# Attention with a mixture of experts: tokens of twelve batches loaded a second time in squares and turned by VectorE, with the norm moved into weights and copies

## The chip, the cores and the metric

One core of one Trainium2 chip. The metric is the device time of one execution in microseconds. The engines named below are TensorE (PE; its weight loads are PEld), VectorE (DVE), ScalarE (ACT), GpSimd (POOL) and SyncE (SP), which here only issues transfers.

## What is computed

Tokens x (16 batches of 512 tokens, 128 channels, fp32) are normalised over the channels. The result goes both through causal attention with 16 heads of 8 channels, whose queries and keys are scaled to length one, and through 8 experts of which each token uses the best two. Both are added to x.

```python
xn = (x - mean(x)) / sqrt(var(x) + 1e-5)
# attention
q, k, v = heads(xn @ Wq), heads(xn @ Wk), heads(xn @ Wv)
sim = (l2norm(q) @ l2norm(k).T) * 8.0            # causal
attn = (softmax(sim) @ v) @ Wo
# experts
probs = softmax(xn @ Wr.T); top_v, top_i = top_k(probs, 2)
w_e = where(top_i == e, top_v / sum(top_v), 0)
ffn = sum_e(w_e * (gelu(xn @ W1[e].T + b1[e]) @ W2[e].T + b2[e]))
out = x + attn + ffn
```

## The kernel before

**Order.** From line 1027 on, the instructions of PE, DVE, ACT and SP run in the order in which the program writes them (`manual_schedule`); `on_pool` (line 562) does the same for POOL. What is written before that line (loads of x and of weights, constants) is placed by the scheduler. An engine that waits holds up all that is written behind it on that engine.

**Stages.** The attention of a batch is ten stages (`PER`), 160 in all. `stage` (line 1175) writes for each: the scores of this stage (`scores`, line 725: PE matmuls `sim`, ScalarE exponentials `ex`), one step of the list `side` (line 1141), the causal masks due, the products with v of an earlier stage (`weigh`, line 772, into the PSUM tile `av`), and the steps that `at_stage` has booked for stage t. Preparing a batch (`prep`, line 622) is booked into the stages before it: four projections (`proj`, line 628), squares and their sums, the length (`root`), the scaling, the turns of q and k (`turn_q`, `turn_k`) and the four masked copies of k (`alone`).

**Tokens.** `load_x` (line 100) brings a batch as [128 tokens, 4, 128 channels]; SP issues all sixteen first. `stats` (line 225) takes mean and variance of each token on VectorE, `scales` (line 252) makes `rstd` and `shift`, and `normalise` (line 289) writes `rows`, the normalised tokens, on ScalarE or GpSimd. Matmuls need them with channels on the partitions: `turn_x` (line 302) turns four 128x128 blocks on PE into a PSUM bank, and a copy brings the bank to `xnT[b]`. Batches 0 to 2 are turned ahead of stage 0; `turn(3)` to `turn(15)` are steps of `side` in stages 0 to 18, with VectorE as the copier. `proj` multiplies a block of `xnT[b]` with `wall` (Wq, Wk and Wv side by side) and lets ScalarE copy the result to `qkv`. `logits` (line 311) multiplies `xnT` of four batches with `wr_sb`, and VectorE copies the result to `ltT`; `turn_logits` turns it back and writes `lg`. `logits(0)` is the sixth step of `side`, `logits(4)` the eighth. `rows` is also what GpSimd later scatters into `slots`, the expert's input, from stage 40 on.

**Buffers.** `misc` (line 191) is one PSUM bank shared by turns, projections, logits and others. `SIM` uses one of three double banks. `scratch` (line 220) hands out two SBUF buffers in turn; its users are, in the order of writing, `count_up` (line 1044), `fill` (line 1071), then `ltT` of `logits(0)`, `ltT` of `logits(4)`, and so on.

**SP's queue.** After the sixteen loads of x, SP issues 45 stores of the tile `fill` to `slots` in HBM (line 1075), 24 copies that pack the experts' weights (line 1084), the store and load of the counts (line 424), and from line 865 on, for each block of the experts, four loads `z<-slots` and one `w<-packed`. `z` is loaded in squares: tokens 32 at a time on 32 partitions, pieces of 32 channels, 128 bytes each, so that VectorE's transpose of 32x32 squares turns it (`turn_rows`, line 882).

**Idle work.** `keep_busy` (line 1058) lets PE do matmuls on a tile of zeros.

```python
    def scratch(name, n):

        return rs.tile([P, NB * E], F32, tag="scratch", name=name, bufs=2)[:, :n]
```

Of the kernel before, what the change touches and what calls it, by code (L numbers as in the profile page):

```python
# [10 lines left out]
F32 = mybir.dt.float32  # L11
I32 = mybir.dt.int32
AF = mybir.ActivationFunctionType
ALU = mybir.AluOpType
# [10 lines left out]
def attention_moe_kernel(  # L25
# [19 lines left out]
    nc = tc.nc  # L45
    B, S, D = x.shape
    E = wrT.shape[1]
    M = w1T.shape[2]
    P = 128
    NC = S // P  # L50
# [3 lines left out]
    TB = 32  # L54
    NQKV = 3 * D
    NG = 4
    GB = 4
# [4 lines left out]
    NT = B * NC  # L62
# [15 lines left out]
    for k in range(E - 1):  # L78
# [9 lines left out]
    keep = ctx.enter_context(tc.tile_pool(name="keep", bufs=1))  # L88

    xnT2 = [  # L90
        keep.tile([P, 2, S], F32, tag=f"xnT{b}", name=f"xnT{b}") for b in range(0, B, 2)
    ]
# [7 lines left out]
    def load_x(b):  # L100
        t = keep.tile([P, NC, D], F32, tag=f"x{b}", name=f"x{b}")
        nc.sync.dma_start(t, x[b].rearrange("(c p) d -> p c d", p=P))
        x_sb.append(t)

    wall = const.tile([P, NQKV], F32, name="wall")
    wr_sb = const.tile([P, 32], F32, name="wr_sb")
# [5 lines left out]
        nc.scalar.dma_start(wall[:, n * D : (n + 1) * D], w)  # L112
    nc.scalar.dma_start(wo_sb, wo)
    nc.scalar.dma_start(b1_sb, b1T)
    for b in range(B):
        load_x(b)

# [45 lines left out]
        channel_multiplier=0,  # L165
    )

    xnT = [xnT2[b // 2][:, b % 2] for b in range(B)]

    pos = keep.tile([P, 2, NT], I32, name="pos")  # L170

# [19 lines left out]
    def misc(name):  # L191
        return ps_m.tile([P, 512], F32, tag="misc", name=name)

    def SIM(name):
        return ps_sim.tile([P, 2, S], F32, tag="sim", name=name)[:, 0]
# [4 lines left out]
    ]  # L200


    rctx = ExitStack()
    rs = rctx.enter_context(tc.tile_pool(name="rs", bufs=1))
    rows_all = rs.tile([P, NT, ROW], F32, name="rows")
    rows = [rows_all[:, b * NC : (b + 1) * NC] for b in range(B)]
    lg = rs.tile([P, NT, E], F32, name="lg")
    wsel = rs.tile([P, 2, NT], F32, name="wsel")
    sels = [rs.tile([P, NT, E], F32, tag=f"sel{k}", name=f"sel{k}") for k in range(2)]
    st = rs.tile([P, NT, 6], F32, name="st")  # L210
    rstd = rs.tile([P, NT], F32, name="rstd")
    shift = rs.tile([P, NT], F32, name="shift")
    ones = rs.tile([P, P], F32, name="ones")
    upper = rs.tile([P, P], F32, name="upper")
# [74 lines left out]
    def normalise(b, engines):  # L289

        for c, engine in enumerate(engines):
            i = b * NC + c
            to, what = rows[b][:, c, :D], x_sb[b][:, c]
            by, less = rstd[:, i : i + 1], shift[:, i : i + 1]
            if engine is nc.scalar:
                nc.scalar.activation(to, what, AF.Identity, bias=less, scale=by)
            elif engine is nc.vector:
                nc.vector.tensor_scalar(to, what, by, less, ALU.mult, ALU.add)
            else:
                on_pool(nc.gpsimd.tensor_scalar, to, what, by, less, ALU.mult, ALU.add)  # L300

    def turn_x(b, bank, copy):

        for c in range(NC):
            nc.tensor.transpose(bank[:, ts(c, P)], rows[b][:, c, :D], ident)
        copy(xnT[b], bank)  # L306


    turned = {}

# [10 lines left out]
    def turn_logits(b0):  # L321
        ltT = turned.pop(b0)
        pt = misc(f"lg{b0}")
        for c in range(NC):
            nc.tensor.transpose(pt[:, ts(c, P)], ltT[:, ts(c, P)], ident)
        nc.vector.tensor_copy(
            lg[:, b0 * NC : (b0 + GB) * NC].rearrange("p (g c) e -> p c g e", g=GB),
            pt.rearrange("p (c g w) -> p c g w", g=GB, w=32)[:, :, :, :E],
        )

    def route():

# [289 lines left out]
    def prep(b):  # L622

        t0 = PER * b
        s = live[b] = {}
        s["vaug"] = vaugs[b % 2]

        def proj(c, bank=misc):
            if not c:
                s["qkv"] = p2.tile([P, NC, NQKV], F32, tag="qkv", name=f"qkv{b}")  # L630
            pp = bank(f"proj{b}_{c}")
            nc.tensor.matmul(  # L632
                pp[:, :NQKV], xnT[b][:, ts(c, P)], wall, start=True, stop=True
            )
            nc.scalar.copy(s["qkv"][:, c], pp[:, :NQKV])  # L635

        heads = lambda t: t.rearrange("p c (h d) -> p c h d", d=DH)

        def squares(c):
            if not c:  # L640
                s["qkn"] = p1.tile([P, NC, 2 * D], F32, tag="qkn", name=f"qkn{b}")
            qk = s["qkv"][:, c, : 2 * D]
            on_pool(nc.gpsimd.tensor_mul, s["qkn"][:, c], qk, qk)

        def values(c):
            on_pool(
                nc.gpsimd.tensor_copy,
                s["vaug"][:, c : c + 2, :, 0:DH],
                heads(s["qkv"][:, c : c + 2, 2 * D : 3 * D]),
            )  # L650

        n = NC * 2 * HEADS

        def sums():
            s["ss"] = sm.tile([P, n], F32, tag="ss", name=f"ss{b}", bufs=1)
            nc.vector.tensor_reduce(
                s["ss"].rearrange("p (c h) -> p c h", c=NC), heads(s["qkn"]), AX.X, ALU.add
            )
            nc.vector.tensor_scalar_max(s["ss"], s["ss"], L2_EPS * L2_EPS)

        def root_now(meanwhile):

            s["rn"] = sm.tile([P, n], F32, tag="rn", name=f"rn{b}", bufs=1)
            nc.scalar.activation(s["ss"], s["ss"], AF.Sqrt)
            meanwhile()
            nc.vector.reciprocal(s["rn"], s["ss"])

        def root():

            s["rn"] = sm.tile([P, n], F32, tag="rn", name=f"rn{b}", bufs=1)  # L670
            (by_log if b < B - 1 else guess)(s["rn"], s["ss"])

        def root_step():
            t = sm.tile([P, n], F32, tag="t", name=f"t{b}")
            refine(s["rn"], s["ss"], t, 1 if b < B - 1 else 3)

        def scale():
            nc.vector.tensor_mul(
                heads(s["qkn"]),
                heads(s["qkv"][:, :, : 2 * D]),  # L680
                s["rn"].rearrange("p (c h) -> p c h", c=NC).unsqueeze(3).to_broadcast(
                    [P, NC, 2 * HEADS, DH]
                ),
            )

        def turn_q():
            pt = misc(f"qt{b}")
            for c in range(NC):
                nc.tensor.transpose(pt[:, ts(c, P)], s["qkn"][:, c, :D], ident)  # L689
            s["qT"] = p2.tile([P, S], F32, tag="qT", name=f"qT{b}")  # L690
            nc.vector.tensor_copy(s["qT"], pt)

        def turn_k(bank=misc):
            pt = bank(f"kt{b}")
            for c in range(NC):
                nc.tensor.transpose(pt[:, ts(c, P)], s["qkn"][:, c, D:], ident)  # L696
            s["kr"] = p1.tile([P, S], F32, tag="turned", name=f"kr{b}")
            nc.vector.tensor_copy(s["kr"], pt)

        def alone(r):  # L700

            if not r:
                s["kT"] = p2.tile([P, NG, S], F32, tag="kT", name=f"kT{b}")
            nc.vector.tensor_scalar_mul(s["kT"][:, r], s["kr"], hmask[:, r : r + 1])  # L704

        if not b:
            return SimpleNamespace(
                proj=proj, squares=squares, values=values, sums=sums, root_now=root_now,
                scale=scale, turn_q=turn_q, turn_k=turn_k, alone=alone,
            )  # L710
        times = (-18, -17, -14, -11) if b > 1 else (-11, -11, -10, -9)
        for c, t in enumerate(times):
            at_stage(t0 + t, lambda c=c: proj(c, SIM if t0 + t < 0 and c else misc))
        for t, step in (
            (-11, lambda: squares(0)), (-11, lambda: squares(1)),
            (-10 + (b == 1), lambda: squares(2)), (-9 + (b == 1), lambda: squares(3)),
            (-8, lambda: values(0)),
            (-7, lambda: values(2)), (-7, sums), (-6, root),
            (-5, root_step), (-4, scale), (-3, turn_q), (-2, turn_k),
            (-2, lambda: alone(0)), (-1, lambda: alone(1)), (0, lambda: alone(2)),  # L720
            (b != B - 1, lambda: alone(3)),
        ):
            at_stage(t0 + t, step)
# [321 lines left out]
    first = 0  # L1045
# [12 lines left out]
    def keep_busy(n, what=spare):  # L1058

        for _ in range(n):  # L1060
            nc.tensor.matmul(
                misc("idle")[:, : what.shape[1]], what[:, :P], what, start=True, stop=True
            )

    keep_busy(4)
    stats(0)
    for step in scales(0, 1, True):
        step()
# [3 lines left out]
    nc.gpsimd.memset(fill, 0.0)  # L1072
    nc.gpsimd.memset(fill[:, :, D : D + 1], float(2 * T))
    for k in range(NFILL):
        nc.sync.dma_start(
            slots[k * P * NR : (k + 1) * P * NR].rearrange("(p r) w -> p r w", r=NR),
            fill,
        )
# [11 lines left out]
    ACT, POOL, DVE = nc.scalar, nc.gpsimd, nc.vector  # L1090
    zero = prep(0)
    normalise(0, (ACT, ACT, DVE, DVE))
    turn_x(0, SIM("xnt0"), nc.scalar.copy)
    for b in range(1, 4):
        stats(b)
# [40 lines left out]


    def turn(b):
        turn_x(b, misc(f"xnt{b}"), nc.vector.tensor_copy)

    side = [
        lambda step=step, b=b: step(b)
# [88 lines left out]
    t = PER * B  # L1231
# [48 lines left out]
```

## Time and profile before

| | us |
|---|---|
| median of 3 runs | 757.83 |
| lowest, highest | 748.12, 759.42 |
| the profiled execution | 759.72 |
| its span in the trace | 757.9 |

| engine, in the whole span | busy us | instructions |
|---|---|---|
| TensorE | 718.6 | 6270 |
| VectorE | 478.1 | 1066 |
| ScalarE | 468.1 | 732 |
| GpSimd | 458.3 | 545 |

The chain of waits is read from its last instruction back: at each step to what released it, so its lines are where the time of the whole went. A line of a timeline or of the chain begins with the start and the length in microseconds. In a table by windows each line has the stretch, its length, the busy time of PE, PEld, DVE, ACT and POOL with the number of instructions, the granted PE clock, the mean busy share of the 16 DMA engines and the rate in GB/s; the share can pass 1 when packets of one engine overlap. `SPq` or `DVEq` is the sequencer of an engine, which also shows semaphore waits. The stages of attention run from about 24 us to 440 us and again from about 690 us; between lie the blocks of the experts.

### The profile page before, as it was taken

How to read it: one execution, taken by the hardware profiler on the slowest of the kernel's cores; microseconds unless marked ns; L12 is line 12 of the kernel's file. 1: busy time of each engine (PE TensorE's matmuls, PEld its weight loads, DVE VectorE, ACT ScalarE, POOL GpSimd, SP SyncE). 2: the span in 40 equal slices, each digit the busy share in tenths (PEclk: the TensorE clock that was granted, in tenths of full speed). 3: DMA queues.
4: the chain of work that ended last, by engine and by line, in shares of the span. 5: the costliest groups of instructions: out<-in, count | busy, mean ns of one | idle time of the engine just before them, and what ended most of it. 6: DMA issues, size and time to landing. Idle time of an engine off the chain costs nothing.

```text
span 757.9 us, 16860 instructions
## 1 busy us (share of the span) xinstructions
PE 718.6 (95%) x6270; PEld 431.9 (57%) x6270; DVE 478.1 (63%) x1066; ACT 468.1 (62%) x732; POOL 458.3 (60%) x545
## 2 busy tenths in 40 slices
PE   8899999999999899998999997999989999999996
PEld 3344444343444344443443476898989999989442
DVE  8855679888777577564675753545455444544487
ACT  4777687777778477776786752444434444344873
POOL 5667455489888587785778423555545555546453
PEclk9999999999999899998999998999999999999999
DMA  9993000010110011110101398999988999893793
GB/s 263 336 266 107 1 2 1 3 37 31 37 37 29 30 34 33 34 37 23 37 30 34 68 160 196 250 252 253 244 215 227 236 244 239 236 238 105 230 339 108
DMA packets 145939, 100.07 MB, mean 132 GB/s; under 512 B 98733, under 2 KB 130608, under 8 KB 145858
## 3 DMA queue, kind: packets, MB, share of 16 engines
q1 hardware_dynamic: 136578, 81.66, 42.5%
q0 software_dynamic: 8416, 17.06, 6.6%
q8 instruction: 50, 0.82, 0.5%
q10 hardware_dynamic: 864, 0.28, 0.2%
q14 instruction: 31, 0.25, 0.1%
HBM read 68.59 MB, written 35.54 MB: 137 GB/s over the span
## 4 chain that ended last, share of the span: by engine, by line
PE 73%; DVE 11%; SPq 4%; POOL 4%; ACT 3%; issue 3%; another core or an unknown queue 1%; DMA 1%; DVEq 0%; ACTq 0%; POOLq 0%
PE sim L735 18%; PE av L922 16%; PE av L779 15%; PE ph L908 13%; PE proj L632 5%; SPq L865 3%; ACT ex L745 2%; DVE x L1016 2%; POOL slots L573 2%; PE po L823 2%; DVE st L227 1%; PE qt L689 1%; DVE mid L791 1%; PE kt L696 1%
## 5 line engine op out<-in xcount | busy, mean ns | idle before, releaser
L745 ACT ACTIVATE ex<-sim 128x1024 f32<-128x1024 f32 x320 | 309.9, 1022 | 108.9 <-PE sim L735 83.9
L573 POOL DMA_INDIRECT results<-y,to x135 | 132.2, 979 | 132.9 <-DVE y L930 98.9
L735 PE MATMUL sim<-qT,kT 32*128 32x512 f32 (+3 forms) x2048 | 199.4, 465 | 5.8 <-ACT ex L745 5.7
L913 ACT ACTIVATE xnT<-ph,bias 128x256 f32<-128x256 f32 x284 | 108.4, 465 | 149.3 <-PE ph L908 102.8
L779 PE MATMUL av<-ex,vaug 128*12 128x512 f32 (+3 forms) x2048 | 171.2, 439 | 8.3 <-DVE mid L791 7.0
L573 POOL TENSOR_SCALAR_AFFINE_SELECT ex<-ex 128x512 f32<-128x512 f32 (+1 forms) x119 | 104.8, 888 | 103.6 <-ACT ex L745 98.4
L573 POOL DMA_INDIRECT slots<-rows,pos x128 | 143.8, 1124 | 31.2 <-issue 29.5
L735 PEld LDWEIGHTS sim<-qT,kT 32*128 32x128 f32 x2048 | 98.5, 184 | 88.4 <-issue 35.6
L908 PE MATMUL ph<-xgT,w 128*128 128x256 f32 (+1 forms) x568 | 131.3, 375 | 8.2 <-DMA w<-packed 5.0
L922 PEld LDWEIGHTS av<-w,xnT 128*128 128x128 f32 x1080 | 132.3, 193 | 10.7 <-ACT xnT L913 5.6
L922 PE MATMUL av<-w,xnT 128*128 128x128 f32 x1080 | 134.6, 278 | 3.8 <-ACT xnT L913 1.4
L779 PEld LDWEIGHTS av<-ex,vaug 128*12 128x12 f32 x2048 | 42.8, 92 | 121.7 <-issue 80.6
L908 PEld LDWEIGHTS ph<-xgT,w 128*128 128x128 f32 x568 | 100.5, 193 | 20.0 <-issue 5.4
L927 DVE TENSOR_TENSOR y<-av,w 128x256 f32<-128x256 f32 x71 | 29.2, 411 | 123.3 <-PE av L922 107.3
L791 DVE STREAM_TRANSPOSE mid<-av 128x512 f32<-128x512 f32 x64 | 45.6, 713 | 70.8 <-PE av L779 46.0
L757 DVE TENSOR_TENSOR ex<-ex,causal 128x1024 f32<-128x1024 f32 (+1 forms) x63 | 68.8, 1092 | 5.5 <-ACT ex L745 5.3
L632 PE MATMUL proj<-wall,xnT 128*128 128x384 f32 x128 | 57.8, 536 | 4.9 <-DVE xnT L306 2.9
L573 POOL TENSOR_TENSOR qkn<-qkv 128x256 f32<-128x256 f32 x64 | 41.4, 657 | 15.0 <-PE kt L696 8.8
L704 DVE TENSOR_SCALAR kT<-kr,hmask 128x512 f32<-128x512 f32 x64 | 37.7, 592 | 0.6
L635 ACT COPY qkv<-proj 128x384 f32<-128x384 f32 x64 | 30.9, 482 | 10.9 <-PE proj L632 6.4
L632 PEld LDWEIGHTS proj<-wall,xnT 128*128 128x128 f32 x128 | 19.4, 188 | 31.8 <-issue 16.2
L886 DVE STREAM_TRANSPOSE xgT<-z 128x256 f32<-128x256 f32 x71 | 30.1, 424 | 6.5 <-DMA z<-slots 6.4
(161 smaller groups left out, 499.0 us busy)
## 6 DMA issues: line engine op xcount, KB each, us to landing
w<-packed SPq DMA_DIRECT2D x71, 576.0 KB
slots<-fill SPq DMA_DIRECT2D x45, 198.0 KB
z<-slots SPq DMA_DIRECT2D x256, 32.0 KB
xnT<-results SPq DMA_DIRECT2D x10, 512.0 KB
x<-in_x_dram SPq DMA_DIRECT2D x16, 256.0 KB
out_dram<-x SPq DMA_DIRECT2D x15, 256.0 KB
yt<-results SPq DMA_DIRECT2D x6, 512.0 KB
results<-y,to POOLq DMA_INDIRECT x135
```

What stands on the lines that cost most here:

```text
L573: ins = op(*args, **kw)
L632: nc.tensor.matmul(pp[:, :NQKV], xnT[b][:, ts(c, P)], wall, start=True, stop=True)
L635: nc.scalar.copy(s["qkv"][:, c], pp[:, :NQKV])
L704: nc.vector.tensor_scalar_mul(s["kT"][:, r], s["kr"], hmask[:, r : r + 1])
L735: nc.tensor.matmul(halves[g // 2][:, g % 2, col : col + (NC - j) * P], s["kT"][group, r, ts(j, P)], s["qT"][group, j * P :], start=True, s ...
L745: nc.scalar.activation(ex[:, 2 * h : 2 * h + 2], half, AF.Exp, scale=SCALE)
L757: nc.vector.tensor_mul(diag, diag, causal.unsqueeze(1).unsqueeze(1).to_broadcast([P, NG, many, P]),)
L779: nc.tensor.matmul(av[32 * g : 32 * g + VW, j * P :], s["vaug"][:, j, NG * g + r], s[m][:, g, col : col + (NC - j) * P], start=(j == 0), s ...
L791: nc.vector.transpose(s["mid"][:, r], av)
L908: nc.tensor.matmul(ph[:, m], s["w1"][:, ts(m, P)], s["xgT"], start=True, stop=True)
L913: nc.scalar.activation(s["gT"][:, m], ph[:, m], AF.Gelu, bias=bias1[:, i, m : m + 1])
L922: nc.tensor.matmul(py[:, c], s["gT"][:, m, ts(c, P)], s["w2"][:, m], start=(m == 0), stop=(m == NM - 1),)
```

## The change

Batches 0 to 3 stay as they were. For batches 4 to 15 (`RAW = GB = 4`), x is loaded once more from HBM, straight into `xnT[b]`, by four transfers for a batch (`load_squares`): each takes 32 channels, lays 32 tokens on 32 partitions, and moves 512 pieces of 128 bytes. Four batches are loaded among the loads of x (after batches 7, 9, 11 and 13), eight between the fills (ahead of every fifth fill, up to the 36th). `turn(b)` becomes one VectorE transpose of `xnT[b]` onto itself, at the same place in `side`.

`xnT` of these batches then holds x as it is. The mean is taken out of the weights: `centre` multiplies `wall` and `wr_sb` with a matrix of ones on PE, and VectorE subtracts the column means, for all batches alike. The scale by `rstd` is put on ScalarE's copies of the projections and on VectorE's copy of the logits. `rstd` moves to a pool that lives on. `normalise` still writes `rows` for all batches.

```diff
+    RAW = GB
+    def load_squares(b):
+        for f in range(D // TB):
+            nc.sync.dma_start(
+                xnT[b][ts(f, TB)].rearrange("p (t f) -> p t f", f=TB),
+                x[b][:, ts(f, TB)].rearrange("(t p) f -> p t f", p=TB),
+            )
+
     for b in range(B):
         load_x(b)
+        if b in (7, 9, 11, 13):
+            load_squares(RAW + (b - 7) // 2)
...
+    rstd = keep.tile([P, NT], F32, name="rstd")
...
+    def turn_raw(b):
+
+        nc.vector.transpose(xnT[b], xnT[b])
+
+    def centre():
+
+        means = SIM("means")
+        for w, first in ((wall, 0), (wr_sb, NQKV)):
+            nc.tensor.matmul(
+                means[:, first : first + w.shape[1]], ones, w, start=True, stop=True
+            )
+        return lambda: [
+            nc.vector.scalar_tensor_tensor(
+                w, means[:, first : first + w.shape[1]], -1.0 / D, w, ALU.mult, ALU.add
+            )
+            for w, first in ((wall, 0), (wr_sb, NQKV))
+        ]
...
-        nc.vector.tensor_copy(
-            lg[:, b0 * NC : (b0 + GB) * NC].rearrange("p (g c) e -> p c g e", g=GB),
-            pt.rearrange("p (c g w) -> p c g w", g=GB, w=32)[:, :, :, :E],
-        )
+        if b0 < RAW:
+            nc.vector.tensor_copy(to, what)
+        else:
+            by = rstd[:, b0 * NC : (b0 + GB) * NC].rearrange("p (g c) -> p c g", g=GB)
+            nc.vector.tensor_mul(
+                to, what, by.unsqueeze(3).to_broadcast([P, NC, GB, E])
+            )
...
-            nc.scalar.copy(s["qkv"][:, c], pp[:, :NQKV])
+            if b < RAW:
+                nc.scalar.copy(s["qkv"][:, c], pp[:, :NQKV])
+            else:
+                i = b * NC + c
+                nc.scalar.activation(
+                    s["qkv"][:, c], pp[:, :NQKV], AF.Identity, scale=rstd[:, i : i + 1]
+                )
...
-    keep_busy(4)
+    keep_busy(3)
+    centred = centre()
     stats(0)
...
     for k in range(NFILL):
+        if k % 5 == 0 and k // 5 < B - 2 * RAW:
+            load_squares(2 * RAW + k // 5)
         nc.sync.dma_start(
...
     normalise(0, (ACT, ACT, DVE, DVE))
+    centred()
     turn_x(0, SIM("xnt0"), nc.scalar.copy)
...
     def turn(b):
-        turn_x(b, misc(f"xnt{b}"), nc.vector.tensor_copy)
+        if b < RAW:
+            turn_x(b, misc(f"xnt{b}"), nc.vector.tensor_copy)
+        else:
+            turn_raw(b)
```

More of the change, by code (lines that the diff above doesn't have):

```diff
@@ L114, in attention_moe_kernel @@
     nc.scalar.dma_start(b1_sb, b1T)
+    RAW = GB
+    xnT = [xnT2[b // 2][:, b % 2] for b in range(B)]
+    def load_squares(b):
[4 more added lines that the diff above has]
+            )
     for b in range(B):
         load_x(b)
+        if b in (7, 9, 11, 13):
+            load_squares(RAW + (b - 7) // 2)
     dram = ctx.enter_context(
@@ L166, in attention_moe_kernel @@
     )
-    xnT = [xnT2[b // 2][:, b % 2] for b in range(B)]
     pos = keep.tile([P, 2, NT], I32, name="pos")
@@ L210, in attention_moe_kernel @@
     st = rs.tile([P, NT, 6], F32, name="st")
-    rstd = rs.tile([P, NT], F32, name="rstd")
     shift = rs.tile([P, NT], F32, name="shift")
@@ L325, in turn_logits @@
             nc.tensor.transpose(pt[:, ts(c, P)], ltT[:, ts(c, P)], ident)
-        nc.vector.tensor_copy(
-            lg[:, b0 * NC : (b0 + GB) * NC].rearrange("p (g c) e -> p c g e", g=GB),
-            pt.rearrange("p (c g w) -> p c g w", g=GB, w=32)[:, :, :, :E],
-        )
+        to = lg[:, b0 * NC : (b0 + GB) * NC].rearrange("p (g c) e -> p c g e", g=GB)
+        what = pt.rearrange("p (c g w) -> p c g w", g=GB, w=32)[:, :, :, :E]
+        if b0 < RAW:
[5 more added lines that the diff above has]
+            )
     def route():
```

## The prediction

> **What bounds the kernel now.** I read the page first: the share of each engine, then the chain that ended last, then the 40 slices.
>
> ```profile
> PE 718.6 (95%) x6270; PEld 431.9 (57%) x6270; DVE 478.1 (63%) x1066; ACT 468.1 (62%) x732; POOL 458.3 (60%) x545
> PE 73%; DVE 11%; SPq 4%; POOL 4%; ACT 3%; issue 3%; another core or an unknown queue 1%; DMA 1%; DVEq 0%; ACTq 0%; POOLq 0%
> DMA  9993000010110011110101398999988999893793
> ```
>
> TensorE is the bound: 95% busy and 73% of the chain. So whatever PE is spared counts, and whatever makes PE wait counts fully. The DMA row shows the second resource: in the first three and a half slices (to about 65 us) it is full with loads of x, fills of `slots` and the packing of weights. The change puts its new transfers exactly there. Next, the chain of waits around the steps that are touched, and the table by windows:
>
> ```profile
> 48.05 1.00 PE lt L315 x8
> 49.04 0.86 PE av L779 x8
> 49.90 0.61 PE qt L689 x4
> ...
> 54.82 0.60 PE xnt L305 x4
> 55.42 0.02 issue
> 55.44 0.70 DVE xnT L306
> 56.15 0.04 issue
> 56.19 0.91 PE proj L632 x2
> ```
>
> A turn costs PE 0.60 us, and one turn in a few makes the next projection wait for VectorE's copy, because both use the single `misc` bank. At 49 us PE runs without a gap from `lt` to `qt`. What stands between them on VectorE decides this case: the copy `ltT<-lt` of the second logits (L319). Its tile is a `scratch` buffer. `scratch` has two, handed out in turn: count_up, fill, ltT0, ltT4. So ltT4 takes the buffer of `fill`, and this copy waits until all 45 stores `slots<-fill` have landed. The view of line L319 in the window 45 to 50 shows the wait, and VectorE's timeline the copy:
>
> ```profile
> L319 DVEq EVENT_SEMAPHORE  x4: 50/50/994, 46.2 to 47.5; - x4
> 49.11 0.69 DVE L319 COPY ltT<-lt 128x512 f32<-128x512 f32 x1 [1.09 <-PE lt L315]
> ```
>
> VectorE's sequencer stood 994 ns at one of its four semaphore waits, and the last of them began at 47.5; VectorE itself then waited for PE. I put the landing of the last fill at 47.3 us, with under 2 us of slack.
>
> **The change part by part.**
>
> Removed: the turns of batches 4 to 15 on PE, 12 x 4 transposes, 12 x 0.59 = 7.1 us, and their waits for VectorE. The four of batches 4 to 7 lie before the point at 49 us, the eight of 8 to 15 after it. The latter give 8 x 0.59 = 4.7 us, and before the projections at 56.19 and 66.19 PE idled 0.23 and 0.72 us for the copy. I take 5.3 of these 5.65.
>
> VectorE: a copy 128x512 from PSUM (667 to 692 ns) becomes a transpose in place in SBUF. The nearest row is L818, 128x512 from SBUF, 702 ns. Equal, so nothing.
>
> Projections: 48 ScalarE copies 128x384 (481 ns) become activations with a scale per partition. Rows L296 (128x128 with two such operands, 492 ns) and L745 (128x1024, 1024 ns) put one at about 0.6 us, so 48 x 0.12 = 5.8 us of ScalarE, which is 62% busy; PE waits for it in places (5.7 us in all at L735). Between 0 and 3 us I take 1.0.
>
> Weights: one matmul in place of one idle matmul, and two VectorE operations of about 0.5 and 0.2 us at 8 us, before the next stats. That is 0.7 us on VectorE, which is the chain there; so are the savings of turns 4 to 7 and the new multiply by `rstd` in the logits (0.29 us copy now; nearly the same). All that comes before 49 us is swallowed by the wait below, so I count none of it; without that wait it would be -0.7 and up to +2.4 us of gain.
>
> Added: 48 transfers of 512 packets of 128 B on SP's queue, 2048 packets a batch. All of them stand ahead of the last fill: 16 among the loads of x, 32 between the fills (the last in front of fill 36 of 45). SP's issue time is not the limit: `z<-slots`, the nearest row, 448 ns median each, so 1.8 us a batch; with the 16 loads (507 ns) and 45 fills (400 ns) 48 us of issue in all, which would end near 49 us. The DMA engines are. Windows of the trace (columns before the end: PE clock, mean DMA share, GB/s):
>
> ```profile
> 2.00:4.00 2.00, 1.94 (x3) 0.37 (x3) 1.35 (x7) 0.00 (x0) 2.00 (x12) 1.00 0.87 258
> 6.00:16.00 10.00, 9.20 (x26) 3.96 (x26) 9.35 (x42) 5.45 (x14) 4.77 (x10) 1.00 1.21 292
> 40.00:44.00 4.00, 4.00 (x44) 1.45 (x44) 2.44 (x9) 3.61 (x8) 1.43 (x3) 1.00 1.01 336
> 433.20:434.80 1.60, 1.60 (x16) 0.73 (x12) 1.04 (x2) 1.28 (x2) 0.19 (x1) 1.00 0.46 66
> 450.00:453.00 3.00, 3.00 (x23) 2.82 (x22) 1.29 (x5) 1.52 (x4) 1.49 (x3) 1.00 1.88 27
> ```
>
> At 433 us only `z` loads run, pieces of 128 B of rows in HBM, the same form as the squares: 66 GB/s is 516 packets a us, and 16 x 0.46 / 516 = 14.3 ns of an engine for each. Loads of x (512 B) have 27.6 ns each when they begin (2 to 4 us) and pass one per 28.1 ns and engine when the queue is full (292 GB/s), so the first kind of number gives the second. `told` (16 B) passes one per 9.5 ns; the straight line from 16 B to 512 B gives 13.7 for 128 B. I take 14.3: a batch is 128 packets per engine, 1.83 us, and twelve are 22.0 us.
>
> A rule of the Trainium skill for this packet: "DMA: Bandwidth & Descriptors", section "Why small descriptors are slow (HBM only)", says that a packet costs its 32-byte beats plus about 3 cycles. For 128 B against 512 B that is 7 to 19, and with 28.1 ns for the latter 10.4 ns. By it a batch is 1.33 us and the twelve 16.0. The trace's row has the very form, so I keep 22.0 and the rule is my low end. The high end is the load of the expert phase: from 500 to 540 us, share 0.97 and 11 blocks, an engine-time of 56.4 us a block; less the weights (590 KB at the 336 GB/s of the fills: 28.1) and two scatters (q0's 6.6% over 263: 3.0 each) leaves 22.3 us for 1024 packets, 21.8 ns each, 33.5 us for twelve.
>
> Nothing else waits for the squares. By the same rates those of batch 7 have come at about 22 us (turned at 39), and the later ones lie ahead of the last fill. Were they late, VectorE's transposes would wait, but L319 has waited already. Queued behind the squares on SP are the fills and the packing, which ends near 87 us in place of 65 and is first read at 428; the `counts` store waits for VectorE at 124. POOL's queue gains nothing.
>
> The wait: last fill at 47.3 + 22.0 = 69.3 us; then the copy ltT (0.7) and `qt` at 70.1 in place of 49.9. Behind the copy in VectorE's order stand qT, the logits, kr and kT, and PE's next instruction but one, `qt`, needs the bank that this copy frees. So PE stands from about 49 to 70 us: **+20.2**.
>
> After a stand PE is slow. The timeline of PE:
>
> ```profile
> 456.82 1.84 PE L922 MATMUL av<-w,xnT 128*128 128x128 f32 x15
> 463.62 3.75 PE L908 MATMUL ph<-xgT,w 128*128 128x256 f32 x8 [4.96 <-DMA w<-packed]
> ```
>
> After 4.96 us of waiting the eight matmuls took 3.75 us, against 1.89 for the same eight at 451 us. "TensorE: Matmul & The Clock Gate", section "Part 1: The HAM clock gate", has half the clock after an idle window of 3.4 us, until as long a busy one has passed. That speaks against this change: +1.9 by the row, +1.7 by the rule, and 0 if one counts the stand alone. I take 1.9.
>
> Sum: 20.2 - 5.3 + 1.0 + 1.9 = **+17.8 us**. The profiled execution took 759.7 (span 757.9), 1.9 above the median of 757.8; so 777.5 for a like execution, and **776** against the median. The three runs lie 11 us apart, so some us of any outcome are chance.
>
> **The rivals.**
>
> First, faster: the fills land before VectorE gets to L319, or the wait is short. Then 7.1 us on PE, about 2 of waits, less 1.0 and 0.7: -7, 751 us. For it: the issue time would allow it. It decides where the delay (the twelve batches less 1.8 us) equals the later savings of 4.3: at 6.1 us for the twelve, 0.5 us each; but 262 KB at the full 336 GB/s take 0.78. Against it are the bytes alone; it needs the buffer rotation to be other than I read it.
>
> Second, no change that can be told: packets overlap better than at 433 us, 0.8 to 1.6 us a batch, as the rule above allows. The sum then runs from +5 to +15, 763 to 773 us. For it: small packets show shares up to 1.88, so that several are under way at once.
>
> Third, the change spares PE nothing after 49 us because ScalarE's longer copies hold the bank: the 5.3 goes and the cost is 3, total +25, 783 us. Against it: ScalarE is busy 14 of 19 us in these windows.
>
> Fourth, packets at 21.8 ns in the full queue: +29, 787 us.
>
> **How the numbers follow.** What a measurement of this kernel can tell from no change is about 2%, here 15.2 us. Chances: forecast (12 to 20 ns a packet) 0.60, packets cheaper 0.19, faster rival 0.07, third and fourth together 0.14. The threshold of +15.2 is met at 12.6 ns a packet, so nearly all of the forecast's part and the last two count as slower: 0.68; the second rival and a remainder are within 2%: 0.25; faster by over 2% needs the first rival and luck besides: 0.07. The range goes from the low end by the rule (+12, less some us of scatter) to the high end (+29 and some): 763 to 790.
>
> **What would show it.** In the chain of waits of the changed kernel, a `DMA slots<-fill` (or an unnamed queue) of some 20 us before `ltT` near 48 us, PE's slices 3 and 4 of 40 nearly empty, a DMA row full to about 87 us, and the first matmuls after the gap at half speed. From `qt` on, the stages to 95 us shorter by about 5 us. Wrong, if `ltT` waits for PE as now, if the last fill lands under 60 us, or if VectorE waits at the new transposes for their squares.

## The result and the profile after

| | kernel before | changed kernel |
|---|---|---|
| median of 4 runs, us | 753.19 | 793.47 |
| lowest, highest | 748.12, 759.42 | 789.78, 797.09 |
| the profiled execution (span) | 759.72 (757.9) | 797.09 (795.4) |

The changed kernel takes 1.0558 times as long (95% interval 1.0442 to 1.0675): about 40 us more, where 18 were forecast. (The median of the kernel before has a fourth execution in it, of 748.55 us.) The page of the changed kernel, with the same rows as before:

```profile
PE 713.6 (90%) x6224; PEld 429.6 (54%) x6224; DVE 479.2 (60%) x1068; ACT 471.9 (59%) x732; POOL 455.2 (57%) x545
PE   4009999999999989999899999899999999999996
PEclk9558999999999998999899999999999999999999
DMA  9989300000100110101010139999997989895595
PE 66%; SPq 12%; DVE 9%; DMA 3%; issue 3%; ACT 3%; POOL 2%; another core or an unknown queue 1%; ACTq 0%; DVEq 0%; POOLq 0%
```

PE is busy for 5.0 us less in all: the removed turns (7.1 us by the prediction's count) less some 2 us by which its first matmuls after the long stand are slower. But the second and third slices of the span (20 to 60 us) hold none of its work. The DMA row is full for longer. So there is one long stand, and it begins at 12 us where the prediction had one from 49: not behind the logits of stage 7, but ahead of stage 0. The timelines of PE show where, the kernel before first, the changed kernel second; the view of who waited for whom in the changed kernel gives the releaser:

```profile
12.32 2.20 PE L1061 MATMUL idle<-xnT 128*128 128x512 f32 x4
```

```profile
9.43 2.85 PE L668 MATMUL proj<-wall,xnT 128*128 128x384 f32 x8 [0.68 <-ACT xnT L319]
58.79 4.18 PE L1103 MATMUL idle<-xnT 128*128 128x512 f32 x4 [46.52 <-DMA xnT<-in_x_dram]
62.76 1.06 PE L318 MATMUL xnt<-ident,rows 128*128 128x128 f32 x4
...
67.34 0.63 PE L731 MATMUL qt<-ident,qkn 128*128 128x128 f32 x4
```

```profile
PE idle L1103 <- DMA xnT<-in_x_dram: 46.5, 1, 46.5
PE av L821 <- DVE mid L833: 8.0, 9, 2.3
PE sim L777 <- ACT ex L787: 5.9, 8, 1.1
```

The instruction that waits is an idle matmul. `keep_busy` reads `spare`, and `spare` is not a tile of its own: it is `xnT2[-1][:, 0]`, the half of `xnT` that belongs to batch 14, cleared at the start. In the kernel before, the first to write there is the copy behind the turn in stage 17. In the changed kernel `load_squares(14)` writes there, and it stands in the program ahead of the idle matmuls behind the first projections. They therefore read what the load brings, and wait for it. (The line in which `spare` is made is the same in both kernels.) SP's timeline of the changed kernel, around that load:

```profile
51.62 2.57 SPq L1120 DMA_DIRECT2D slots<-fill  x5
54.30 2.43 SPq L122 DMA_DIRECT2D xnT<-in_x_dram  x4
56.77 2.59 SPq L1120 DMA_DIRECT2D slots<-fill  x5
59.40 2.38 SPq L122 DMA_DIRECT2D xnT<-in_x_dram  x4
61.83 5.64 SPq L1120 DMA_DIRECT2D slots<-fill  x10
67.51 0.67 SPq L1129 DMA_DIRECT2D packed<-in_w1T_dram  x1
```

Batch 14's four transfers, the last but one group of squares, are issued from 54.30 to 56.73 us, and PE goes on at 58.79. The work that these matmuls do has no use for the result; the wait is for a clearing that the load has overwritten.

The wait that was forecast does not show. VectorE's timeline of the changed kernel, at the copy `ltT` of `logits(4)`:

```profile
94.51 0.69 DVE L350 COPY ltT<-lt 128x512 f32<-128x512 f32 x1 [1.14 <-PE lt L346]
```

It waits for PE, as before: when PE comes here at 94 us, the last fill (issued before 67.51) has long landed. Still, its tile is that of `fill`, as the prediction read it. VectorE's sequencer passes four semaphore waits ahead of the first copy that takes the tile of `fill`; in the kernel before they stood at 46.2 to 47.5 us, ahead of `ltT` of `logits(4)`, one of them for 994 ns, and here they stand at the same copy and cost nothing:

```profile
L350 DVEq EVENT_SEMAPHORE  x4: 50/50/50, 91.6 to 91.8; - x4
```

### The profile page after: what moved, and what is told of

It reads as the page before. It is cut to its first block, busy times and chain, and to the rows that moved or that the text cites. A ratio compares the mean times of both kernels' runs of the same rounds, so it can differ in the third digit from the quotient of the medians.

```text
span 795.4 us, 16844 instructions
## 1 busy us (share of the span) xinstructions
PE 713.6 (90%) x6224; PEld 429.6 (54%) x6224; DVE 479.2 (60%) x1068; ACT 471.9 (59%) x732; POOL 455.2 (57%) x545
## 4 chain that ended last, share of the span: by engine, by line
PE 66%; SPq 12%; DVE 9%; DMA 3%; issue 3%; ACT 3%; POOL 2%; another core or an unknown queue 1%; ACTq 0%; DVEq 0%; POOLq 0%
PE sim L777 18%; PE av L821 15%; PE av L964 13%; PE ph L950 11%; PE proj L668 5%; SPq L122 4%; SPq L907 3%; ACT ex L787 3%; SPq L1120 3%; DVE x L1058 2%; PE po L865 1%; DMA z<-slots 1%; PE qt L731 1%; DMA w<-packed 1%; DVE mid L833 1%
## 5 line engine op out<-in xcount | busy, mean ns | idle before, releaser
L609 POOL DMA_INDIRECT slots<-rows,pos x128 | 141.4, 1105 | 31.3 <-issue 29.9
L1103 PE MATMUL idle<-xnT 128*128 128x512 f32 x16 | 12.6, 882 | 48.3 <-DMA xnT<-in_x_dram 46.5
L609 POOL TENSOR_SCALAR rows<-x,rstd,shift 128x128 f32<-128x128 f32 x41 | 18.7, 467 | 53.9 <-DVE shift L296 53.8
L733 DVE COPY qT<-qt 128x512 f32<-128x512 f32 x16 | 11.0, 690 | 58.2 <-PE qt L731 56.6
```

Of the source, the lines that this page charges most:

```text
L609: ins = op(*args, **kw)
```

## The experiments

The eight kernels below ran apart from the pair above, in two groups on two chips, each with its own runs of the kernel before, which takes 728 us there; so ratios are compared. The second group is e5 to e8. None of them is the changed kernel itself; `e3_ltT` stands in for it there, at a ratio of 1.0532 (its interval lies inside that of 1.0558).

### e1_spare: the idle matmuls read another half

```diff
-    spare = xnT2[-1][:, 0]
+    spare = xnT2[1][:, 1]
```

> The changed kernel, with the idle matmuls reading the zeros in the half of batch 3 (which is never loaded in squares) in place of batch 14's. Theory A (the idle matmul at 12 us waits for the squares of batch 14; that stand of 46.5 us is where the loss comes from, and it hid a second wait that the prediction named): PE no longer stands at 12 us, and VectorE's copy ltT of logits(4) now waits for the last fill, which lands near 72 us; about +19 us on the kernel before, 770 to 776 us. Rival B (the stand is the only wait; the second does not exist): the time falls below the kernel before, about 746 us. Rival C (the loss is the DMA load itself and PE would stand somewhere for as long): stays near 793 us.

Measured: 722.77 us, ratio 0.9921 (0.9901 to 0.9941). One line takes away the whole loss, and the change becomes a gain of 0.8%. Theory A was right about the first wait and wrong about the second; rival B, without a second wait, was right, and rival C is out. The copies `ltT` and the last fills in this kernel, from the timelines of VectorE and SP:

```profile
48.61 0.69 DVE L350 COPY ltT<-lt 128x512 f32<-128x512 f32 x1 [1.41 <-PE lt L346]
66.04 0.69 DVE L350 COPY ltT<-lt 128x512 f32<-128x512 f32 x1 [1.73 <-PE lt L346]
84.20 0.69 DVE L350 COPY ltT<-lt 128x512 f32<-128x512 f32 x1 [1.01 <-PE lt L346]
```

```profile
61.63 2.32 SPq L122 DMA_DIRECT2D xnT<-in_x_dram  x4
63.99 5.65 SPq L1120 DMA_DIRECT2D slots<-fill  x10
69.69 0.67 SPq L1129 DMA_DIRECT2D packed<-in_w1T_dram  x1
```

The copies at 48.61 and 66.04 start before the last fill is even issued, and wait for PE alone. So neither writes the tile of `fill`. In the built program of this kernel all four `ltT` take the other buffer, and fill's goes to the first step of the routing, `val` at 88.9 us. There the four semaphore waits stand now:

```profile
L382 DVEq EVENT_SEMAPHORE  x4: 50/50/50, 87.9 to 88.2; - x4
88.87 0.69 DVE L382 TENSOR_TENSOR val<-lg,mx 128x512 f32<-128x512 f32 x1
```

In the built programs of the kernel before and of the changed kernel the `ltT` of `logits(4)` takes fill's buffer, as in their traces above. So the buffers of `scratch` are not handed out strictly in turn, and which tile gets which can move with an edit that touches neither. By what rule they are handed out stays open.

### e2_spare_ltT, e3_ltT, e4_before_ltT: the logits off the buffer of fill

To each of e1_spare, the changed kernel and the kernel before, the same edit:

```diff
-        ltT = turned[b0] = scratch(f"ltT{b0}", S)
+        if b0 in (4, 8):
+            ltT = turned[b0] = sels[b0 // 4 - 1].rearrange("p n e -> p (n e)")
+        else:
+            ltT = turned[b0] = scratch(f"ltT{b0}", S)
```

> As the run before, and the copies ltT of logits(4) and logits(8) go to tiles that are free until the routing (sel0, sel1), so that neither takes the buffer of fill. Theory A: no stand is left; 7 us under the kernel before, 744 to 749 us, and the squares are never late (batch 8's land near 28 us, batch 15's near 64, their turns start near 50 and 80). Rival B: the same as the run before. Rival D (a third wait, VectorE for late squares, takes over): a line of VectorE's transpose waiting for xnT, and a time above the kernel before.

> The changed kernel with only the copies ltT moved off the buffer of fill; the idle matmuls still read batch 14's half. Theory A: the same as the changed kernel, 790 to 797 us, since the last fill lands before PE is back at the logits. If the two waits added up it would fall by some 20 us.

> The kernel before with only the copies ltT moved off the buffer of fill. All theories: within 1% of the kernel before (there the last fill had landed before VectorE came to the copy). It is the control for the runs with moved copies.

| | us | ratio (interval) |
|---|---|---|
| e2_spare_ltT | 723.34 | 0.9918 (0.9896 to 0.9939) |
| e3_ltT | 767.28 | 1.0532 (1.0513 to 1.0551) |
| e4_before_ltT | 728.04 | 0.9999 (0.9984 to 1.0013) |

e2 equals e1: there was no wait left to take away, so e2 met its number for a reason that its theory did not give. e3 still stands 47.4 us at the idle matmul. The control changes nothing. So the loss of the changed kernel is the one wait of PE.

### e7_swap and e8_no_idle: is it these matmuls, and these squares

In the changed kernel, batch 14's squares change places with batch 8's; and, separately, the five idle matmuls behind the first projections are left out:

```diff
-            load_squares(2 * RAW + k // 5)
+            load_squares((14, 9, 10, 11, 12, 13, 8, 15)[k // 5])
```

```diff
-    keep_busy(2)
...
-    keep_busy(2)
...
-    keep_busy(1)
```

> The changed kernel with the squares of batches 14 and 8 in exchanged places between the fills; the idle matmuls still read batch 14's half. Theory A (they wait for exactly these squares): batch 14's are issued from 28 us and land near 32 in place of 58.8, so that the stand of PE at 12 us shrinks from 46.5 to about 19 us; the time falls by about 27 us from 767, to 737 to 744. If the stand were for the queue as a whole (any of its transfers), no change.

> The changed kernel without the five idle matmuls behind the first projections (keep_busy of 2, 2 and 1); no other edit. Theory A: no stand, since nothing reads batch 14's half before its turn; as e1_spare, plus up to 3 us where PE's clock falls in the gaps: 722 to 727 us. If PE waited for the squares in another place, near 767.

e7_swap: 738.84 us, ratio 1.0141 (1.0113 to 1.0169). Its timelines of PE and of SP:

```profile
29.30 4.18 PE L1103 MATMUL idle<-xnT 128*128 128x512 f32 x4 [17.02 <-DMA xnT<-in_x_dram]
```

```profile
24.20 2.16 SPq L122 DMA_DIRECT2D xnT<-in_x_dram  x4
```

Batch 14's squares are issued 30 us earlier, PE's stand shrinks from 46.5 to 17.0 us, and the time falls by 28 us against e3. The length of the stand follows the place of this one load in the queue. (No copy `ltT` adds a wait here: the four semaphore waits stand at 99.6 us, ahead of the last of them, 50 ns each.)

e8_no_idle: 723.84 us, ratio 0.9947 (0.9929 to 0.9966). Without the idle matmuls nothing waits; PE's gaps before stage 0 then are up to 3.06 us long, and from 19 to 24 us PE's granted clock is 0.50, where e1_spare has 1.00. The kernel ends 0.3% above e1_spare, some 2 us, but the two intervals touch. So the five idle matmuls are worth little, some 2 us; where they waited they cost 44.5 us (e3_ltT less e1_spare).

### e5_in_fill: the forecast wait, made by hand

e1_spare with `ltT` of `logits(4)` in the tile of `fill`:

```diff
-    turned = {}
+    turned, held = {}, []
...
-        ltT = turned[b0] = scratch(f"ltT{b0}", S)
+        ltT = turned[b0] = held.pop() if b0 == 4 else scratch(f"ltT{b0}", S)
...
-    fill = scratch("fill", NR * ROW).rearrange("p (r w) -> p r w", w=ROW)
+    filled = scratch("fill", S)
+    held.append(filled)
+    fill = filled[:, : NR * ROW].rearrange("p (r w) -> p r w", w=ROW)
```

> e1_spare (idle matmuls off batch 14's half), and the copy ltT of logits(4) is put by hand into the tile of fill, where the prediction had it. Theory A' (the second wait did not appear in e1_spare because the buffers are not handed out strictly in turn, and ltT of logits(4) got the other one; the mechanism of the prediction holds where the tile is shared): VectorE waits at that copy from about 48 us to the landing of the last fill, about 73 us; PE stands some 24 us and is slow for 2 more; 745 to 751 us where e1_spare had 723, and the last fill lands as the prediction said, 22 to 26 us later than before. Rival (fills and squares overlap so far that the wait is short): under 735 us.

Measured: 748.77 us, ratio 1.0279 (1.0257 to 1.0301). From the timelines of VectorE and of PE:

```profile
73.53 0.69 DVE L350 COPY fill<-lt 128x512 f32<-128x512 f32 x1 [25.89 <-DMA packed<-in_w1T_dram]
```

```profile
48.72 1.25 PE L821 MATMUL av<-ex,vaug 128*12 128x512 f32 x6
74.28 1.11 PE L731 MATMUL qt<-ident,qkn 128*128 128x128 f32 x4 [24.32 <-DVE fill L350]
75.33 2.09 PE L777 MATMUL sim<-qT,kT 32*128 32x512 f32 x8
```

VectorE waits 25.9 us (the trace names a packing copy issued right behind the last fill) and PE 24.3. With the tile shared, the wait is where the prediction had it. After the stand `qt` took 1.11 us and the next `sim` 2.09, where the timeline of the kernel before has 0.66 and 1.14; from 74 to 78 us the granted clock is 0.52. So PE lost 1.4 us to its clock in these two groups. The stand and this loss together are the 26 us that lie between e1_spare and e5_in_fill.

### e6_copy: the price of the scale on ScalarE

e1_spare with `nc.scalar.copy` for all projections.

> e1_spare with ScalarE's plain copies of the projections in place of activations with a scale; leaves out the scale by rstd of queries, keys and values of batches 4 to 15. It prices the term of the prediction for the longer copies (1.0 us, 0 to 3): 720 to 723 us, against 723 for e1_spare.

Measured: 722.25 us, ratio 0.9919 (0.9901 to 0.9938), the same as e1_spare. Groups of instructions of e1_spare from 0 to 330 us (mean ns in the second place behind the bar):

```profile
L675 ACT ACTIVATE qkv<-proj,rstd 128x384 f32<-128x384 f32 x35 | 20.4, 582 | 0.3
L672 ACT COPY qkv<-proj 128x384 f32<-128x384 f32 x16 | 7.6, 482 | 4.7 <-PE proj L668 4.7
```

An activation with a scale per partition takes 100 ns more than the copy. On 48 of them that is 4.8 us of ScalarE. What of it lies on the path can't be told from nothing: the intervals of the two ratios are 0.2% to each side, 1.4 us.

## Why the prediction was wrong

**The step that failed** is the sentence "Nothing else waits for the squares." The prediction followed the new transfers to the readers that the change names (the turns, the logits) and to what is queued behind them on SP. It did not ask who else reads the tiles that they write. `spare` reads one, under another name. The stand of 46.5 us is that omission; its size is the place of batch 14 in the queue (e7_swap). It goes when the idle matmuls read another tile (e1_spare) and when they are left out (e8_no_idle).

**The forecast wait** is a second step that failed, in two ways. In the changed kernel its premise held, `ltT` of `logits(4)` has fill's tile, but the stand had delayed that copy past the landing of the last fill. Without the stand the premise failed: "`scratch` has two, handed out in turn" (the section on the kernel before says the same), and in e1_spare `logits(4)` does not take fill's tile. Its mechanism and price hold where the tile is shared by hand (e5_in_fill). Against a forecast of +17.8 us on the kernel before, e5_in_fill has +21 (748.77 less 727.54). That +18 and +40 have the same sign is no merit of the prediction: it named another tile, another instruction and another place. One of the signs by which it called itself wrong was met: `ltT` waits for PE as before.

**Terms of the sum**, by what they measured:

| term | forecast | measured |
|---|---|---|
| twelve batches of squares, us until the last fill | 22.0 | 24.5 (first packing copy issued at 67.51, before at 43.02); 25.6 in e1_spare (69.69, 44.07 in e4_before_ltT) |
| a batch, per packet and engine | 14.3 ns | 24.5 / 12 / 128 = 16.0 ns, if the engines set the pace |
| saving of the turns of batches 8 to 15 | 5.3 us | 4.6 (from the second to the fourth `ltT`: 40.23 us in e4_before_ltT, 35.59 in e1_spare) |
| ScalarE's scale | 1.0 us | not told from none (e6_copy) |
| PE's clock after a stand of over 20 us | 1.9 us | 1.4 in the two groups of e5_in_fill |
| VectorE's transpose in place | as the copy | 699 ns in place of 691; it never waited for its squares |

If all of the delay is put down to the packets, they were 12% dearer than the row of `z`, far above the estimate of 10.4 ns that the prediction worked out from the Trainium skill ("DMA: Bandwidth & Descriptors", "Why small descriptors are slow (HBM only)"), and below the 21.8 of the high end. But it is not shown that the engines set the pace. The prediction's "SP's issue time is not the limit" rested on 448 ns an issue; a square took SP 530 ns in the changed kernel, and 48 of those are 25.4 us, as much as the whole delay. From 38 to 57 us the DMA engines were at a share of 0.90, where the fills by themselves had 1.01. An issue may itself take longer because the engines are behind, so no run here separates the two.

The granted clock was 0.50 from 19 to 57 us of the changed kernel, inside the stand, and the first group of idle matmuls after it took 4.18 us where the kernel before has 2.20. The rule on the clock gate in the Trainium skill ("TensorE: Matmul & The Clock Gate", "Part 1: The HAM clock gate"), half the clock after an idle window, agrees with both.

**The first rival**, faster by 7 us, is what the change does without the collision: 5 us (727.96 less 722.77). It had been put at 7% because the wait at `ltT` seemed sure; the prediction said of it that it "needs the buffer rotation to be other than I read it", and so it was. In e1_spare the second `ltT` comes 0.73 us sooner than in e4_before_ltT (48.61, 49.34); with the 4.6 us between the second and the fourth that is the gain. The 40 us of the result close as well: the first `qt`, ahead of stage 0, began at 19.89 us and now begins at 67.34, 47.5 later; the fourth `ltT` at 129.68 in place of 89.36, 40.3 later. Between them lie the twelve turns, 7.1 us by the prediction's count, about the difference.

**The version to keep** is e1_spare, 0.8% faster than the kernel before (interval 0.6 to 1.0%). That the order of squares and fills could be better still was not tried.

## What to carry to other kernels

When a change lets a load write into memory that was free until now, list every reader of that memory under every name, those whose result is thrown away too: an idle matmul that reads borrowed zeros becomes a dependency on the load, and holds an in-order engine. Where a wait rests on which buffer of a rotating pool a tile gets, read it from the built program of that very version, since an edit elsewhere can move it. And a wait that is found first may not be the one that counts: follow each engine's own waits from its first instruction on.

## What the runs showed of the hardware

Loads of 128-byte pieces of rows in HBM kept the sixteen engines at a mean share of 0.90 to 0.99 and 233 to 250 GB/s together with the fills (19 to 57 us of the changed kernel); fills by themselves ran at 336 GB/s (40 to 44 us of the kernel before). Twelve batches of squares delayed SP's queue by 24.5 us, 0.51 us for each transfer of 512 pieces. SP spent 0.53 us to issue 512 of them, against 0.45 us for 256 of `z`. A transpose of 128x512 in place took VectorE 699 ns, and a copy of that size from PSUM 691. On ScalarE an activation with a scale per partition took 582 ns at 128x384, the plain copy 482. The idle matmuls before stage 0 keep the granted clock at 1.00 from 19 to 24 us, where it is 0.50 without them; that is worth some 0.3% of this kernel (e8_no_idle against e1_spare; the intervals touch).
